# Expert outputs scattered to token order and summed per batch inside the next attention, in a four-layer decoder

## The chip, the cores and the metric

The kernel runs on one NeuronCore of a Trainium2 chip. The time is device time in microseconds for one execution of the whole program, from its first to its last instruction on that core.

## The reference, cut to what matters

The model is a decoder of four layers with layer norm after each sublayer: x = layernorm(x + f(x)) twelve times, for x of 8 batches, 256 tokens and width 256. In layers 0, 1 and 2 the sublayers are self attention, cross attention and a feed-forward network with experts. The change is about the experts of layers 0 and 1 and the attentions that follow them. Layer 0 sends each token to one of 8 experts and weights the result with the expert's softmax probability:

```python
sel = expert_idx == e
out = out + jnp.where(sel, expert_w, 0.0)[:, None] * y
```

Layer 1 sends each token to four of 32 experts. An expert takes at most C = 256 tokens; a choice that finds its expert full counts as zero. A shared expert is added.

```python
slot = jnp.minimum(pos, C)
expert_out = jnp.pad(expert_out, ((0, 0), (0, 1), (0, 0)))
gate = jnp.where(pos < C, w_s, 0.0)[:, None]
routed = jnp.zeros_like(x).at[t_s].add(expert_out[e_s, slot] * gate)
shared = _silu_and_mul(x @ shared_w_gate_up) @ shared_w_down
return (routed + shared).reshape(b, s, h)
```

## The kernel before

**Tiling.** The 2048 tokens are 16 tiles of 128 (NT = 16); a batch is two tiles. The residual X lies in SBUF as [128, 16, 256], beside xT, its transpose, from which the projections read. `finish(i)` closes a sublayer for the two tiles i and i+1: statistics (L163, L164), reciprocal square root, the normalised X (L187), four transposes on TensorE (L173) and a copy into xT by ScalarE (L174). The reciprocal square root is two POOL operations (L141, L143) within the attentions and cross attentions, where a flag `power` is set, and eleven tiny VectorE operations (L146 to L154, three Newton steps) within the expert layers.

**Order.** The program is written engine by engine through a tile framework with pools of buffers; a scheduler decides the order in which instructions stand on each engine, and inserts the waits. On each engine, instructions run in that order. Weights of the next sublayer are loaded one sublayer ahead into two tiles that alternate.

**l0_ffn** (lines 920 to 1015). After routing, tokens are grouped by expert into at most 23 blocks of 128 slots. Before it, in l0_xattn, X was written to a DRAM table `xd` by ScalarE's DMA queue (L851), batch by batch. For each block: POOL gathers the block's expert weights `we` (2.1 MB, two buffers) and its 128 token rows `xe` by indirect DMA (`gather_rows`, L893); TensorE multiplies; VectorE adds the bias to give `y` (L1005); SP writes `y` to the DRAM table `yd` in slot order (L1006). When all blocks are written, a second loop over the tiles gathers `yg`, the row of each token, from `yd` by POOL, weights it and adds X on VectorE (L1012), and calls `finish`.

**l1_ffn** (lines 1120 to 1195). `route1` (L1030 to 1117) makes `take`, the token of each expert's slot, by small matmuls against one-hot tables (`own`, `at`, `found`), and `slot`, the slot of each token's choice. Then the 32 experts: SP loads `we` (L1159, 384 KB), POOL gathers two tiles `xe`, TensorE transposes and multiplies, VectorE copies `y` (L1176), SP writes it to `yd` (L1177). `prepare_l2_xattn`, work for a later sublayer, is placed among the experts by the scheduler. When all experts are written, a loop over the 16 tiles adds the shared expert's product `py` to X (`acc`, L1187), gathers four `yg` rows per token by POOL and adds each with its weight on VectorE (L1192), and calls `finish` for two tiles at a time.

**attention16** (L593 on) runs l1_attn and l2_attn batch by batch: `pair(b)` projects two batches (`turned` L777 in l1_attn for rotary positions; `qv`, `kv`, `vp`), `largest16` finds score maxima (`low`, reductions on VectorE, L462 and L478), `lower16` (L497, L499) subtracts them, then exponentials on ScalarE, sums and output.

## Time and profile before

| | us |
|---|---|
| median of 3 runs | 2801.1 (2792.59 to 2802.07) |
| the profiled execution | 2675.02 |
| its span, first to last instruction | 2673.2 |
| PE, DVE, ACT, POOL busy | 2156.6, 1678.8, 957.6, 890.1 |

The profiled execution is 126 us shorter than the median of the three timed runs; its mean granted TensorE clock is 0.883. All stage times below are of that one execution. In the profile, PE is TensorE, DVE VectorE, ACT ScalarE, POOL GpSimd and SP the engine that only issues DMAs. A group row names line, engine, operation, output and inputs, the count, the busy time and the mean of one, then the engine's idle time just before such instructions and what ended most of it. A row of waits names the waiting engine and line, what it waited for, total us, times, and the longest. Stages by their first and last instructions: l0_ffn's blocks 332 to 557.6, its gathers and norms to 594, l1_attn from there; l1_ffn's experts 1026 to 1173.4, its gathers to 1257, l2_attn from there.

### The profile page before, as it was taken

What the parts mean: (1) busy time and instruction counts of PE and PEld (TensorE: products, weight loads), DVE (VectorE), ACT (ScalarE), POOL (GpSimd) and SP (SyncE); (2) the same over time, 40 slices, a digit from 0 to 9 for tenths busy, and PEclk for the clock granted to TensorE, in tenths of its full rate; (3) what the DMA queues carried; (4) which work ended last, traced back from release to release, by engine and by line L of the source; (5) the groups of instructions that cost most, each with busy time, mean ns of one, the idle gap of its engine ahead of it and who ended that gap; (6) DMA issues with size and microseconds to landing.
All of it is one profiled execution on the core that took longest, in us unless ns stands there. A gap on an engine that the chain in (4) does not pass through costs nothing.

```text
span 2673.2 us, 40915 instructions
## 1 busy us (share of the span) xinstructions
PE 2156.6 (81%) x14331; PEld 1560.5 (58%) x14331; DVE 1678.8 (63%) x5710; ACT 957.6 (36%) x2197; POOL 890.1 (33%) x949
## 2 busy tenths in 40 slices
PE   8978688869999867854998667888898899878975
PEld 5555477745556546741555425666677677656754
DVE  4754400056666757536676788787797787664876
ACT  2321133323333344211344224345455445433431
POOL 1021121131111112446111003776767766670000
PEclk9998599989998877985999788898999998887987
DMA  2001276720001013743000001212111211220000
GB/s 84 2 1 36 88 255 242 268 76 1 1 1 68 13 43 99 229 147 87 1 1 25 36 0 60 54 52 53 51 48 46 59 46 50 54 75 0 1 20 12
DMA packets 84172, 166.28 MB, mean 62 GB/s; under 512 B 31653, under 2 KB 51253, under 8 KB 80256
## 3 DMA queue, kind: packets, MB, share of 16 engines
q0 software_dynamic: 52288, 110.51, 13.5%
q1 hardware_dynamic: 28924, 49.45, 5.5%
q10 hardware_dynamic: 2756, 3.72, 0.4%
q8 instruction: 114, 1.87, 0.3%
q14 instruction: 90, 0.74, 0.1%
HBM read 242.90 MB, written 17.70 MB: 97 GB/s over the span
## 4 chain that ended last, share of the span: by engine, by line
PE 20%; DVE 17%; DMA 6%; issue 5%; POOL 2%; ACT 2%; POOLq 0%; ACTq 0%; DVEq 0%
DMA rows<-in_l2f_table_dram,index 6%; PE s L132 3%; PE pp L132 3%; PE po L1392 3%; PE po L132 3%; DVE junk L1340 2%; DVE low L478 1%; POOL rows L893 1%; PE ph L132 1%; PE sc L132 1%; PE s L1538 1%; PE sc L445 1%; PE s L1516 1%; DVE X L187 1%; DVE top_i L1216 1%
## 5 line engine op out<-in xcount | busy, mean ns | idle before, releaser
L893 POOL DMA_INDIRECT rows<-in_l2f_table_dram,index x512 | 531.9, 1039 | 227.7 <-issue 68.9
L1340 DVE SCALAR_TENSOR_TENSOR junk<-rows,X 128x256 f32<-128x256 f32 x512 | 215.8, 421 | 145.7 <-DMA rows<-in_l2f_table_dram,index 134.6
L1392 PE MATMUL po<-rows,diag 128*128 128x256 f32 x768 | 218.5, 423 | 43.6 <-ACT diag L1391 41.6
L132 PE MATMUL ph<-xeT,we 128*128 128x128 f32 x1248 | 187.4, 294 | 35.2 <-DMA we<-in_l0f_experts_dram,wrow 31.0
L132 PEld LDWEIGHTS ph<-xeT,we 128*128 128x128 f32 x1248 | 172.8, 204 | 58.5 <-DMA we<-in_l0f_experts_dram,wrow 34.4
L1392 PEld LDWEIGHTS po<-rows,diag 128*128 128x128 f32 x768 | 149.0, 207 | 91.3 <-ACT diag L1391 65.0
L553 POOL TENSOR_TENSOR aT<-sides,inv 128x256 f32<-128x256 f32 x64 | 46.7, 730 | 448.4 <-DVE sides L551 255.8
L132 PE MATMUL pp<-xT,w 128*128 128x256 f32 (+1 forms) x672 | 183.4, 411 | 9.6 <-DVE hT L1028 3.3
L173 PE MATMUL pt<-ident,X 128*128 128x128 f32 x352 | 77.7, 335 | 119.7 <-DVE X L187 105.5
L1391 ACT ACTIVATE diag<-ident,dots 128x128 f32<-128x128 f32 x384 | 133.1, 394 | 103.0 <-DVE dots L1386 62.7
L893 POOL DMA_INDIRECT xe<-xd,take x87 | 85.0, 977 | 221.7 <-DVE y L1005 94.7
L132 PEld LDWEIGHTS pp<-xT,w 128*128 128x128 f32 x672 | 131.9, 203 | 40.2 <-issue 9.4
L174 ACT COPY xT<-pt 128x512 f32<-128x512 f32 x88 | 51.5, 586 | 277.0 <-PE pt L173 276.7
L1005 DVE TENSOR_TENSOR y<-py,we 128x256 f32<-128x256 f32 x23 | 9.8, 425 | 220.3 <-PE py L132 220.3
L141 POOL TENSOR_SCALAR rs_v<-ln_mv 128x2 f32<-128x2 f32 x48 | 12.4, 259 | 389.2 <-DVE ln_mv L164 358.5
L173 PEld LDWEIGHTS pt<-ident,X 128*128 128x128 f32 x352 | 50.2, 165 | 156.7 <-issue 73.3
L132 PE MATMUL py<-we,hT 128*128 128x256 f32 x496 | 132.2, 391 | 0.9 <-DVE hT L1028 0.9
L517 ACT ACTIVATE e<-sc 128x512 f32<-128x512 f32 (+1 forms) x155 | 82.0, 602 | 105.5 <-PE sc L445 92.2
L999 ACT ACTIVATE hT<-ph,we 128x128 f32<-128x128 f32 x184 | 66.0, 367 | 142.8 <-PE ph L132 136.0
L187 DVE TENSOR_SCALAR X<-z,ln_mv,rs_y 128x256 f32<-128x256 f32 x192 | 72.0, 418 | 52.2 <-POOL rs_y L143 52.1
L445 PE MATMUL sc<-kv,qv 32*128 32x128 f32 (+2 forms) x1448 | 101.5, 320 | 2.8 <-DVE sides L551 0.8
L445 PEld LDWEIGHTS sc<-kv,qv 32*128 32x128 f32 x1448 | 78.3, 190 | 37.4 <-issue 30.1
(489 smaller groups left out, 5223.5 us busy)
## 6 DMA issues: line engine op xcount, KB each, us to landing
we<-in_l1f_experts_dram SPq DMA_DIRECT2D x32, 384.0 KB, 4.2
yd<-y SPq DMA_DIRECT2D x32, 256.0 KB, 2.1
rows<-in_l2f_table_dram,index POOLq DMA_INDIRECT x512, 2.8
w<-in_l2x_w_dram SPq DMA_DIRECT2D x1, 4096.0 KB
yd<-y SPq DMA_DIRECT2D x23, 128.0 KB, 1.7
X<-in_x_dram SPq DMA_DIRECT2D x8, 256.0 KB, 7.7
xd<-X ACTq DMA_DIRECT2D x8, 256.0 KB, 2.2
xd<-X SPq DMA_DIRECT2D x8, 256.0 KB, 2.1
```

Of the source, the lines that this page charges most:

```text
L132: self.nc.tensor.matmul(out, lhsT=lhsT, rhs=rhs, start=n == 0, stop=n == last and bias is None)
L173: nc.tensor.transpose(pt[:, c, j, :], self.X[:, i0 + j * step, c * P : (c + 1) * P], self.ident)
L174: nc.scalar.copy(self.xT4[:, :, i0 : i0 + step + 1 : step, :], pt)
L187: nc.vector.tensor_scalar(self.X[:, i, :], z[:, j, :], mv[:, j, 0:1], r[:, j : j + 1], ALU.subtract, ALU.mult)
L445: nc.tensor.matmul(sc[: shape[0], part], lhsT=lhsT, rhs=rhs, start=mask is None, stop=True, skip_group_check=True)
L517: lambda r, sc: nc.scalar.activation(e0[m][:n0, r], sc, AF.Exp),
L553: nc.gpsimd.tensor_tensor(out, split(both), split(inv), ALU.mult)
L893: self.nc.gpsimd.indirect_dma_start(out=out, out_offset=None, in_=table, in_offset=bass.IndirectOffsetOnAxis(ap=index, axis=0), **({} if r ...
L999: nc.scalar.activation(hT[:, g + f, :], ph[:, f, :], AF.Gelu, bias=b1[:, g + f : g + f + 1])
L1340: nc.vector.scalar_tensor_tensor(junk, row, 1.0, self.X[:, i, :], ALU.mult, ALU.mult, accum_out=out)
L1391: nc.scalar.activation(diag, self.ident, AF.Copy, scale=dots[:, k : k + 1])
L1392: nc.tensor.matmul(po, lhsT=diag, rhs=rows[:, k, D:], start=False, stop=g + k == H * K - 2)
```

## The change

The two tables of results are now laid out by token and choice: yd0 has a row per token, yd1 four rows per token. In both expert layers each `y` is scattered to its rows by POOL as soon as it exists. The slots that hold no token get an index beyond the table, and are dropped by a bounds check. The index `put` comes from `take`; in layer 1 the number of the choice is added, for which `own` gets a third table and `found` a third column. SP's writes of `y` and the loops of gathers go away. In l1_ffn the shared expert is added to X in eight steps (L1250 after). The weighted sums and `finish` move into the attention that follows: `ready(b)` loads a batch's rows in order with one DMA (256 KB in l1_attn with three buffers, 1 MB in l2_attn with two), adds them on VectorE (L978 after; two operations a batch in l1_attn, eight in l2_attn), and finishes the batch. It is called for batches 0 and 1 ahead of the first projection, for 2 after it, and for b+3 in each batch. As dropped choices leave rows of yd1 unwritten, l1_attn fills yd1 with zeros at its start, by one memset (L786) and 16 DMAs of 512 KB from SP (L788). The expert weights `gw` and the buffers lie in the spare part of the attention's weight tile. Lines of the kernel after differ from those of before: L502 after is L499, L806 is L777, L1089 is the scatter of l0_ffn, L1242 that of l1_ffn.

```diff
@@ class Net
+        self.yd0 = dram.tile([NTOK, D], F32, name="yd0")
+        self.yd1 = dram.tile([NTOK * 4, D], F32, name="yd1")
@@ attention16
+        for b in range(2 if ready else 0):
+            ready(b)
         pair(0)
+        if ready:
+            ready(2)
...
         for b in range(B):
             ahead = []
+            if ready and b + 3 < B:
+                ready(b + 3)
@@ l2_attn
+                ready=self.taken_back(self.yd1, 4, self.gw1, spare, 2, pool_from=8),
@@ l1_attn
+        zero = spare[:, 10 * D :]
+        nc.vector.memset(zero, 0.0)
+        for i in range(NT):
+            nc.sync.dma_start(
+                self.yd1[i * 4 * P : (i + 1) * 4 * P, :].rearrange("(p k) d -> p k d", k=4),
+                zero.unsqueeze(1).to_broadcast([P, 4, D]),
+            )
...
+ready=self.taken_back(self.yd0, 1, self.gw0, spare, 3)
@@ new functions
+    def scatter_rows(self, table, index, src):
+        ins = self.nc.gpsimd.indirect_dma_start(
+            out=table,
+            out_offset=bass.IndirectOffsetOnAxis(ap=index, axis=0),
+            in_=src,
+            in_offset=None,
+            bounds_check=table.shape[0] - 1,
+            oob_is_err=False,
+        ).ins
...
+    def put_index(self, takef, n, keep, per=1, part=None):
+        none = keep.tile([P, n], F32, name="none_at")
+        nc.vector.tensor_scalar(none, takef, 0.5, 1e6, ALU.is_lt, ALU.mult)
+        if part is not None:
+            nc.vector.tensor_tensor(none, none, part, ALU.add)
+        nc.vector.scalar_tensor_tensor(none, takef, float(per), none, ALU.mult, ALU.add)
+        put = keep.tile([P, n], U32, name="put")
+        nc.vector.tensor_scalar(put, none, float(per), 0.0, ALU.subtract, ALU.max)
+        return put
+    def taken_back(self, yd, k, gw, spare, nbuf, pool_from=B):
+        def batch(b):
+            y, z = ys[:, b % nbuf], zs[:, b % 2]
+            nc.sync.dma_start(
+                y, yd[b * S * k : (b + 1) * S * k, :].rearrange("(j p k) d -> p j k d", p=P, k=k)
+            )
+            engine = nc.gpsimd if b >= pool_from else nc.vector
+            for j in range(2):
+                t = 2 * b + j
+                for n in range(k):
+                    acc = z[:, j] if n else self.X[:, t, :]
+                    engine.scalar_tensor_tensor(
+                        z[:, j], y[:, j, n], gw[:, t, n : n + 1], acc, ALU.mult, ALU.add
+                    )
+            self.finish(2 * b, 1, z)
@@ l0_ffn
-                    nc.sync.dma_start(yd[n * P : (n + 1) * P, :], y)
-                for i in range(0, NT, 2):
-                    z = work.tile([P, 2, D], F32, name="z")
-                    for j in range(2):
-                        y = work.tile([P, D], F32, name="yg")
-                        self.gather_rows(y, yd, slot[:, i + j, :])
-                        nc.vector.scalar_tensor_tensor(
-                            z[:, j], y, gw[:, i + j : i + j + 1], self.X[:, i + j, :], ALU.mult, ALU.add
-                        )
-                    self.finish(i, 1, z)
+                    self.scatter_rows(self.yd0, put[:, n : n + 1], y)
@@ route1
+        for k in range(K):
+            nc.scalar.mul(own[:, k, 2], oh[:, k], float(k))
...
+        put = self.put_index(takef, 2 * E, keep, K, choice)
@@ l1_ffn
-                    nc.sync.dma_start(yd[e * C : (e + 1) * C, :].rearrange("(t p) d -> p t d", p=P), y)
+                    for n in range(2):
+                        self.scatter_rows(self.yd1, put[:, n * E + e : n * E + e + 1], y[:, n])
...
-                for i in range(0, NT, 2):
-                    z = work.tile([P, 2, D], F32, name="z")
+                for t in range(0, NT, 2):
+                    po = ps.tile([P, 2, D], F32, name="py")
                     for j in range(2):
-                        t = i + j
-                        po = ps.tile([P, 2, D], F32, name="py")
-                        self.mm(po[:, 0, :], [(shT[:, t * P : (t + 1) * P], sd)])
-                        acc = work.tile([P, D], F32, name="acc")
-                        nc.vector.tensor_tensor(acc, po[:, 0, :], self.X[:, t, :], ALU.add)
-                        for k in range(K):
-                            y = work.tile([P, D], F32, name="yg", bufs=6)
-                            self.gather_rows(y, yd, slot[:, t, k : k + 1])
-                            out = z[:, j] if k == K - 1 else acc
-                            nc.vector.scalar_tensor_tensor(out, y, gw[:, t, k : k + 1], acc, ALU.mult, ALU.add)
-                    self.finish(i, 1, z)
+                        self.mm(po[:, j, :], [(shT[:, (t + j) * P : (t + j + 1) * P], sd)])
+                    x = self.X[:, t : t + 2, :]
+                    nc.vector.tensor_tensor(x, po, x, ALU.add)
```

## The prediction

> **What bounds the kernel now.** I read the span cut into windows first, with the edges at the stages that the change touches: the expert blocks of l0_ffn, what follows them, the expert loop of l1_ffn, its gathers, the start of l2_attn, the rest of it. Columns: start:end length, busy time of each engine with instructions in brackets, granted clock, DMA share, GB/s.
>
> ```profile
> 332.00:557.60 225.60, 192.44 (x1148) 170.84 (x1148) 9.74 (x23) 73.76 (x208) 39.23 (x42) 0.93 0.67 243
> 557.60:578.00 20.40, 3.19 (x9) 1.87 (x10) 13.36 (x70) 1.17 (x2) 11.95 (x13) 0.61 0.27 79
> 1047.40:1173.40 126.00, 108.46 (x758) 95.44 (x756) 63.34 (x121) 29.74 (x91) 55.88 (x59) 0.99 0.73 216
> 1173.40:1257.40 84.00, 24.74 (x61) 12.11 (x59) 49.86 (x190) 3.52 (x6) 60.96 (x64) 0.54 0.36 102
> 1286.00:1480.00 194.00, 162.00 (x1814) 99.64 (x1815) 129.30 (x283) 79.84 (x142) 26.88 (x39) 0.96 0.06 22
> ```
>
> The expert loop is TensorE's: 31 periods from the first y (1047.5) to the last (1173.4), 4.06 us each, PE busy 86%, POOL 44%. The 84 us behind it belong to POOL: 64 gathers, PE nearly idle. The 20 us behind l0_ffn's blocks are the same in small. Next, the groups and waits of that 84 us stretch, to see the price of a gather, and who waits.
>
> ```profile
> L893 POOL DMA_INDIRECT yg<-yd,slot x64 | 61.0, 953 | 31.3 <-DMA yd<-y 12.1 <-issue 5.8 <-DVE rs_y L154 3.0
> L1192 DVE SCALAR_TENSOR_TENSOR acc<-yg,gw,acc 128x256 f32<-128x256 f32 x47 | 22.7, 483 | 31.5 <-DMA yg<-yd,slot 31.0
> ...
> PE pt L173 <- DVE X L187: 37.3, 6, 10.0
> ```
>
> A gather costs 0.95 us busy and 0.30 us between two: 64 x 1.25 = 80 us. VectorE waits 31 us for them, TensorE 37 us for VectorE. Last, a timeline of the expert loop, which tells how long an expert takes from its gather to its y.
>
> ```profile
> 1102.20 0.97 POOL L893 DMA_INDIRECT xe<-xd,take  x1 [1.12 <-DMA xe<-xd,take]
> ...
> 1106.67 0.41 PE L908 MATMUL pt<-ident,xe 128*128 128x128 f32 x2 [1.09 <-DMA xe<-xd,take]
> ...
> 1108.83 0.69 DVE L1176 COPY y<-py 128x512 f32<-128x512 f32 x1 [1.19 <-PE py L132]
> ```
>
> The tile gathered at 1102.20 is transposed at 1106.67, and the y that stands behind this transpose on PE is ready at 1109.5: 7.3 us.
>
> **What the Trainium skill says.** "DMA: Bandwidth & Descriptors", "Anatomy of one DMA — SWDGE (gpsimd) path": about 2.0 us and bytes/436 GB/s, so 2.3 us for 128 KB. The yg gathers land in 2.8 us, xe, beside weight loads, in 3.8 us: more, same order. The same page, "Issuing engines are not separate DMA queues": all DMAs share 16 engines, so the 8.4 MB zero fill takes time from whatever moves then; the trace of before has no such overlap. "SBUF — State Buffer", "SBUF: two separate sides": GpSimd and a VectorE operation with two SBUF inputs can lock each other out. It agrees in tendency: l2_ffn's bounds-checked gathers beside VectorE's two-input L1340 take 1039 ns in the mean, the yg gathers 953.
>
> ```profile
> L893 POOL DMA_INDIRECT rows<-in_l2f_table_dram,index x512 | 531.9, 1039 | 227.7 <-issue 68.9
> ```
>
> **The change, part by part.** (a) Zero fill of yd1: one memset and 16 SP DMAs of 512 KB from about 243 us. SP has nothing else then; DMA is 18% busy over 240 to 300. At the 243 GB/s of the block loop it takes 8.4 MB / 243 = 35 us. ACT's eight xd writes of l0_xattn come among them: in the order built, the last three writes and the zero row wait for the 11th to 13th part of the fill, due near 270 where they issue near 290. Cover: that slack, and xd is first read at 325; behind the fill on SP stand only the weights of l1_xattn. Cost 0; without the cover about 5 us.
>
> (b) l0_ffn's blocks: SP's 23 writes go, 23 scatters come on POOL. No scatter is in the trace of before. Its nearest row is the bounds-checked gather: 0.998 us median plus 0.30, so 1.30. Bounds: 1.25 as a plain gather (no reason for less, it makes the same 128 row addresses), 1.79 from the slowest of those 512 gathers, 1.487 us, and the gap. Each stands before the weight gather of block n+2, which frees a buffer only at y(n) as before; in most blocks the scatter takes the place of an xe gather (1.25) that moves behind it, in the last six or seven it comes on top. Two buffers alternate, so half counts: 6.5 x 1.30 x 0.5 = 4 us; at worst all, 22 x 1.30 x 0.5 = 14; at best 0.
>
> (c) l0 to l1: 16 gathers go; VectorE's Newton steps go too (finish is called inside l1_attn, which takes its root on POOL). Before, the last y is at 557.65 and the first `low` reduction of l1_attn at 607.07. After: y 561.7, scatter and landing 2.8, the 256 KB load 2.2 (as xd's writes of this size), so 567. Then VectorE stands first in line, in the order built: seven batches of two weighted sums (0.48 each), statistics 1.17 and X 0.8, 2.95 a batch, 20.7; turned and vp as before, 6.9; first low at 595. That is -12. The eighth batch's sums and two norms, 5 us, are left inside l1_attn, where I count half of it as hidden: +3. Sum -9, range -14 to +3.
>
> (d) Routing of l1_ffn: four ACT multiplies of 512 numbers come (0.59 each, from ACT's like rows) before 16 that `found` waits for, and a small DVE index computation before the first gather: +2. The five small DVE operations for slots were not on the path.
>
> (e) Expert loop: 32 SP writes go, 64 scatters come. POOL before: 57 gathers x 1.25 = 71 us in 126, waiting for PE. POOL after: per expert 2 x 1.25 + 2 x 1.31 = 5.1 us, over PE's 4.06, so **POOL becomes the bound**. The order built alternates two gathers, two scatters; a scatter waits for y, and behind it stand gathers of the experts two and three ahead. From a gather to the scatter of the y that depends on it POOL has one and a half periods, 7.6 us, of other work; the path is 7.3 us. So it just doesn't lock. From the first y at 1049.5: 28.5 experts x 5.12 = 146, last gather at 1195.5; landing 4, the y in front 2.5, its own expert 4, last y 1206; second scatter issued 1.3 later and landed 2.8 after that: 1210. The loop's end has moved by +35.
>
> (f) l1 to l2: 64 gathers go, eight loads of 1 MB come. Price of one: `we` of 384 KB lands in 4.2, `we` of 2.1 MB in 9.4, so 3 us and 3 us per MB, 6.2. First batch at 1216. X += shared (8 adds, 16 products) runs beside the last scatters. VectorE's order then puts 45 of the 64 weighted sums and five norms before the first `lower16` (L499): 45 x 0.484 = 21.8; 5 x 1.95 = 9.8; projection copies and lows as before, 14.1 busy; 3 for the root on POOL and for loads, which have two buffers. 1216 + 48.7 = 1265, against 1283.4 before: -18. The remaining 19 sums and three norms, 9.2 + 5.9 = 15 us, fall inside l2_attn, where VectorE is 67% busy with `low` on the path: about half hides, +7 (range 2 to 15). (d), (e) and (f): -11.
>
> Sum: -9 - 11 = **-20 us of the profiled execution**, 2675 to 2655. The median of the runs shown is 126 us above that execution, and nothing in the page says where; I carry the difference over unscaled: 2801 - 20 = 2781. If those runs are slower in TensorE's work, the POOL-bound loop hides some of it, a reason for a little more.
>
> **Rivals.** A, the loop stays TensorE's: were the 0.30 between POOL's instructions hidden, an expert would cost POOL 3.9 and the loop stay at 4.06; then the +35 goes, less 3 for the last scatter: 2801 - 20 - 32 = 2749. Against it: the yg gathers show the 0.30 each time. B, VectorE takes it back: the 15 us inside l2_attn all on the path (+8), and the two load buffers starve the sums (+6): 2795. For it: VectorE at 67% there with its reductions in the chain. C, slower, **POOL's period per expert**: the scatter that waits for y holds gathers behind it. The gain is gone at a period of 5.12 + 20/28.5 = 5.8, and the kernel is slower by 0.5% from 6.3. That takes scatters of 1.9 us, or a path from gather to y of 1.5 x 6.3 = 9.5 us in place of 7.3, as scatter writes crowd the 73% busy DMA engines. At 6.6 it gives 2781 + 42 = 2823. That the change doesn't do what it says is excluded for the gathers: they are gone from the order built.
>
> **How the numbers follow.** Forecast 0.43, A 0.15, B 0.22, C 0.20. About 0.5% (14 us) is what a measurement of this kernel can tell from no change. Faster: A, and two thirds of the forecast's own spread, 0.45; same: most of B and the rest, 0.32; slower: C and a tail of B, 0.23. The range reaches near A and near C, leaving out half of A and half of C: 2753 to 2818. The forecast's own range is 2768 to 2796.
>
> **What would show it.** Right: y's period in the expert loop 5.1 to 5.3 with POOL over 90% busy there; scatters of about 1.0 us; last y near 1206; first L499 of l2_attn (L502 after) near 1265; first low of l1_attn near 595; l0_xattn unchanged to 325. Wrong: a period near 4.1 (A) or above 5.8 (C), ACT waiting for the zero fill, or a gap on VectorE before the sums for loads.

## The result, and the profile after

| | before | after |
|---|---|---|
| median, us | 2801.6 (2792.6 to 2811.4, 4 runs) | 2835.2 (2832.9 to 2843.3, 4 runs) |
| ratio | | 1.013 [1.010, 1.016] |
| profiled execution; span | 2675.02; 2673.2 | 2833.34; 2831.6 |

The changed kernel is slower, by 1.3%. The two profiles must not be laid side by side: the kernel before takes 2679 us on some chips and 2804 us on others (medians of 9 to 61 runs on each of five chips: 2679.1 and 2679.3 on two, 2803.9, 2804.7 and 2805.8 on three). By their times, its profile came from the first kind and the timed runs from the second. Each chip was used in one session, so "kind of chip" may stand for something in its surroundings. The kernel before was profiled again on the second kind ("before again", the first experiment), and the stages below compare that profile with the one after. Its span is 137 us longer than in the first profile; 124 of these lie in l2_ffn, which the change doesn't touch: from its first to its last gather 747 us on one kind, 871 on the other. The windows of the kernel after, with its own edges and the columns of the prediction: l0_ffn's blocks, what follows them up to the last load, the expert loop from first to last y, from there to the first `lower16` of l2_attn, and l2_attn.

```profile
332.00:578.20 246.20, 198.11 (x1146) 177.35 (x1145) 9.73 (x23) 72.45 (x207) 60.80 (x62) 0.89 0.58 216
578.20:591.00 12.80, 1.54 (x6) 1.04 (x7) 5.77 (x20) 0.59 (x1) 6.78 (x9) 0.56 0.40 116
1068.20:1255.20 187.00, 130.51 (x766) 112.31 (x764) 65.73 (x122) 30.29 (x91) 121.51 (x122) 0.85 0.45 140
1255.20:1308.50 53.30, 33.65 (x161) 18.78 (x161) 45.08 (x110) 7.58 (x11) 13.35 (x18) 0.76 0.40 143
1310.00:1504.00 194.00, 172.61 (x1840) 105.81 (x1836) 130.35 (x298) 82.52 (x144) 26.98 (x40) 0.93 0.02 7
```

The same stages of the kernel before, on the second kind of chip:

```profile
332.00:558.60 226.60, 191.44 (x1142) 170.19 (x1140) 9.77 (x23) 71.83 (x205) 37.78 (x40) 0.93 0.66 237
1048.20:1178.60 130.40, 110.27 (x759) 97.11 (x757) 64.19 (x122) 29.73 (x91) 56.17 (x59) 0.97 0.73 209
1178.60:1300.40 121.80, 47.54 (x181) 23.99 (x181) 69.88 (x243) 11.51 (x17) 68.36 (x70) 0.59 0.26 72
```

The blocks take 20 us more. The expert loop takes 187 us in place of 130 for the same 32 experts, and POOL, which was to be its bound, is busy only 121.5 of them, 65%; with the 0.30 us between its instructions counted it is taken for 158 of them, 84%. The stretch behind the loop falls from 122 to 53 us. Landmarks from the trace give the whole account; the forecast's column is worked out from its own landmarks (the last y at 1206, `lower16` at 1265, and so on), each less that of before:

| stretch, us | before again | after | difference | forecast |
|---|---|---|---|---|
| l0_ffn, first to last y | 219.1 | 238.4 | +19.3 | +4 |
| to l1_attn's first `low` | 49.4 | 36.6 | -12.8 | -16 |
| l1_attn, its `low` stretch | 354.4 | 367.8 | +13.4 | +3 |
| to l1_ffn's first y | 86.0 | 85.6 | -0.4 | +2 |
| expert loop, first to last y | 130.2 | 186.9 | +56.7 | +31 |
| to the first `lower16` | 121.9 | 53.4 | -68.5 | -50 |
| l2_attn, to its last `low` | 160.1 | 178.6 | +18.5 | +7 |
| rest | | | -5.8 | 0 |
| sum | | | +20.4 | -20 |

By layers: layer 0 (the first three rows) was forecast to gain 9 us and lost 20; layer 1 (the next four) was forecast to gain 10 and lost 6. The profiles differ by 20 us and the medians by 34: the profiled execution of before again took 2812.5 us, 8.5 more than the median of its own runs, and single executions of the kernel after spread over 10 us, of before over 19. The new instructions on the page after:

```profile
L924 POOL DMA_INDIRECT xe<-xd,take x87 | 85.8, 986 | 181.1 <-PE pt L992 118.2
L936 POOL DMA_INDIRECT yd<-y,put x87 | 88.9, 1022 | 111.2 <-DVE y L1088 69.9
```

A scatter (L936) is busy for 1.02 us; with the 0.30 between two instructions, 1.32. The zero fill changed nothing that can be seen: the first y of l0_ffn is at 339.8 after and at 339.4 before.

### The profile page after: what moved, and what is told of

Its sections match the earlier page's. It is cut to its first block, busy times and chain, and to the rows that moved or that the text cites. A ratio compares the mean times of both kernels' runs of the same rounds, so it can differ in the third digit from the quotient of the medians.

```text
span 2831.6 us, 40750 instructions
## 1 busy us (share of the span) xinstructions
PE 2221.4 (78%) x14331; PEld 1612.7 (57%) x14331; DVE 1662.9 (59%) x5530; ACT 962.1 (34%) x2202; POOL 919.6 (32%) x988
## 4 chain that ended last, share of the span: by engine, by line
PE 27%; DVE 16%; issue 5%; another core or an unknown queue 3%; ACT 3%; POOL 2%; DMA 1%; ACTq 0%; POOLq 0%; DVEq 0%
PE po L1449 5%; PE pp L135 5%; PE s L135 4%; PE po L135 3%; DVE junk L1397 1%; PE po L1430 1%; DVE low L481 1%; PE ph L135 1%; PE s L1595 1%; PE s L1573 1%; PE sc L135 1%; DVE w L978 1%; DVE X L190 1%; PE sc L448 1%
## 5 line engine op out<-in xcount | busy, mean ns | idle before, releaser
L1449 PE MATMUL po<-rows,diag 128*128 128x256 f32 x768 | 233.8, 441 | 103.3 <-ACT diag L1448 54.1
L135 PE MATMUL ph<-xeT,we 128*128 128x128 f32 x1248 | 203.2, 312 | 74.0 <-DMA we<-in_l0f_experts_dram,wrow 46.4
L135 PEld LDWEIGHTS ph<-xeT,we 128*128 128x128 f32 x1248 | 190.1, 222 | 99.5 <-DMA we<-in_l0f_experts_dram,wrow 49.3
L1449 PEld LDWEIGHTS po<-rows,diag 128*128 128x128 f32 x768 | 154.8, 216 | 155.1 <-ACT diag L1448 71.5
L135 PE MATMUL pp<-xT,w 128*128 128x256 f32 (+1 forms) x672 | 195.8, 433 | 27.0 <-issue 15.8
L1448 ACT ACTIVATE diag<-ident,dots 128x128 f32<-128x128 f32 x384 | 134.8, 395 | 137.7 <-PE po L1449 56.7
L135 PEld LDWEIGHTS pp<-xT,w 128*128 128x128 f32 x672 | 140.6, 216 | 61.1 <-issue 24.1
L135 PE MATMUL py<-we,hT 128*128 128x256 f32 x496 | 141.1, 412 | 3.4 <-DVE hT L1102 3.4
L936 POOL DMA_INDIRECT yd<-y,put x87 | 88.9, 1022 | 111.2 <-DVE y L1088 69.9
L448 PE MATMUL sc<-qv,kv 32*128 32x128 f32 (+2 forms) x1396 | 102.1, 346 | 0.0
```

The lines of the kernel that those rows point to most:

```text
L135: self.nc.tensor.matmul(out, lhsT=lhsT, rhs=rhs, start=n == 0, stop=n == last and bias is None)
L448: nc.tensor.matmul(sc[: shape[0], part], lhsT=lhsT, rhs=rhs, start=mask is None, stop=True, skip_group_check=True)
L936: ins = self.nc.gpsimd.indirect_dma_start(out=table, out_offset=bass.IndirectOffsetOnAxis(ap=index, axis=0), in_=src, in_offset=None, boun ...
L1448: nc.scalar.activation(diag, self.ident, AF.Copy, scale=dots[:, k : k + 1])
L1449: nc.tensor.matmul(po, lhsT=diag, rhs=rows[:, k, D:], start=False, stop=g + k == H * K - 2)
```

## The experiments

### Before again, and each half alone

`before again` is the kernel before without an edit. `l0 only` keeps the old l1_ffn and l2_attn; `l1 only` keeps the old l0_ffn and l1_attn. Their core edits, against the kernel after:

```diff
 # l0 only: in l1_ffn, as before
-                    for n in range(2):
-                        self.scatter_rows(self.yd1, put[:, n * E + e : n * E + e + 1], y[:, n])
+                    nc.sync.dma_start(yd[e * C : (e + 1) * C, :].rearrange("(t p) d -> p t d", p=P), y)
 # l1 only: in l0_ffn, as before
-                    self.scatter_rows(self.yd0, put[:, n : n + 1], y)
+                    nc.sync.dma_start(yd[n * P : (n + 1) * P, :], y)
```

> The kernel before once more, unchanged. From l2_ffn on the kernel after has the same order of instructions on each engine as the kernel before, yet the profiled executions differ there by 114 us (the rows gathers take 747 us before, 860 us after). If that belongs to the execution and not to the change, this run's profiled execution takes about 2800 us, with 840 to 860 us between the first and the last rows gather, and reaches the first of them near 1652 us. If the change causes it, this run shows 747 us there again and some 2675 us in all.

> The change in layer 0 alone (scatter in the expert blocks of l0_ffn, sums inside l1_attn); layer 1 as before, no zero fill. My theory now: the blocks of l0_ffn lose 20 us (each scatter stands before the next weight gather), their tail gains 13, l1_attn loses some 8: 10 to 15 us slower than before, about 2813. Rival, the prediction on record: blocks lose 4, sum a gain of 9, about 2792.

> The change in layer 1 alone (two scatters per expert, zero fill in l1_attn, sums inside l2_attn); layer 0 as before. My theory now: the expert loop loses 60 us (period 6.0 in place of 4.06), the tail to the first lower16 of l2_attn gains 56, l2_attn loses 19: 20 to 28 us slower than before, about 2825. Rival, the prediction on record: loop loses 31, tail gains about 47, l2_attn loses 7: a gain of 10, about 2791.

Measured, all on one chip of the second kind: before again 2803.96, ratio 0.9999 [0.9976, 1.0022]; l0 only 2817.8, 1.0060 [1.0038, 1.0082]; l1 only 2809.1, 1.0027 [1.0005, 1.0048]. Each half loses, the second less than the 20 to 28 us that were expected, as the stretch behind its loop saves 68 us and not 56. The second kind of chip shows itself in `before again` much as expected, but its first gather of l2_ffn comes at 1669 and not at 1652: the stretch behind the expert loop is 12.5 us longer there too. `l0 only` loses all that l0_ffn and l1_attn lose together (its last y at 576.6, the end of l1_attn's `low` stretch at 980.9, in place of 558.5 and 962.3); `l1 only` has the expert loop of the change, 187.8 us.

### Where l0_ffn's 19 us come from

The order on POOL in one block, after and in `before again` (start, length, engine, line, operation, idle before):

```profile
406.89 0.95 POOL L924 DMA_INDIRECT xe<-xd,take  x1 [11.49 <-PE pt L992]
408.14 1.01 POOL L936 DMA_INDIRECT yd<-y,put  x1 [0.30 <-issue]
409.46 0.98 POOL L924 DMA_INDIRECT we<-in_l0f_experts_dram,wrow  x1 [0.30 <-issue]
```

```profile
400.58 0.94 POOL L893 DMA_INDIRECT xe<-xd,take  x1 [10.44 <-DVE y L1005]
401.83 0.94 POOL L893 DMA_INDIRECT we<-in_l0f_experts_dram,wrow  x1 [0.30 <-ACT hT L999]
```

After a y, POOL used to issue `xe`, then `we`; now the scatter stands between the two. From y(n) to the gather of `we`(n+2) it was 1.7 us in 15 blocks and 0.7 in six; it is 3.0 and 2.0, except in one block: 1.3 more, the price of the scatter (times from the start of y). To test it, `l0 late` issues the scatter of a block behind the weight gather of the block two ahead:

```diff
                     self.gather_rows(we, self.ins["l0f_experts"], wrow[:, n : n + 1])
+                    if n > 1:
+                        self.scatter_rows(self.yd0, put[:, n - 2 : n - 1], ys.pop(0))
...
-                    y = work.tile([P, D], F32, name="y")
+                    y = work.tile([P, D], F32, name="y", bufs=5)
                     nc.vector.tensor_tensor(y, py, b2, ALU.add)
-                    self.scatter_rows(self.yd0, put[:, n : n + 1], y)
+                    ys.append(y)
...
```

> The kernel after, with each scatter of l0_ffn written two blocks later, behind the weight gather of the block that takes over the buffer. If the scatter ahead of that gather is what slows the blocks, they take 219 us again from the first to the last y (238 in after, 219 before) and the kernel some 18 us less than after, about 2817. Rival: the blocks are slower because the scatters' writes share the DMA engines with the weight gathers; then they stay at 238 and the time at 2835.

Measured on a chip of the first kind: 2680.1, ratio 1.0000 [0.9989, 1.0012]. Its blocks take 221.8 us from first to last y, and 0.7 or 1.7 us from y to `we` as before:

```profile
401.33 0.97 POOL L924 DMA_INDIRECT xe<-xd,take  x1 [8.97 <-DVE y L1091]
402.61 0.95 POOL L924 DMA_INDIRECT we<-in_l0f_experts_dram,wrow  x1 [0.30 <-ACT hT L1085]
403.86 1.01 POOL L936 DMA_INDIRECT yd<-y,put  x1 [0.30 <-issue]
```

A kernel below with layer 0 as changed (`fill`) takes 238.8 for them on this kind of chip. So the place of one POOL instruction ahead of a 2.1 MB weight gather costs l0_ffn 17 us. The blocks as they were before take 215.8 us in the profile of before, and 219.0, 221.0 and 221.2 in three kernels below that leave them alone; so the scatter as such costs at most 6 us, and perhaps nothing. The rival, that the scatters' writes crowd the weight gathers, wanted 238. `l0 late` also has more buffers for y, but these are not the cause: in the kernel after all of y's waiting is for TensorE.

```profile
L1088 DVE TENSOR_TENSOR y<-py,we 128x256 f32<-128x256 f32 x23 | 9.8, 425 | 242.6 <-PE py L135 242.6
```

As nothing else differs, this gives an estimate for the kernel after on the first kind, where it was not run: 2680 and 17, 2697 us, some 18 over the kernel before.

### The expert loop: whose time is it?

`sp write` replaces layer 1's two scatters by one SP write in slot order; the loads then read rows of other tokens, so the sums are of other rows. `xe8` gives the gathered rows eight buffers in place of three (in both layers; the text of a later run says four).

```diff
 # sp write
-                    for n in range(2):
-                        self.scatter_rows(self.yd1, put[:, n * E + e : n * E + e + 1], y[:, n])
+                    nc.sync.dma_start(self.yd1[e * C : (e + 1) * C, :].rearrange("(t p) d -> p t d", p=P), y)
 # xe8
-        xe = work.tile([P, D], F32, name="xe")
+        xe = work.tile([P, D], F32, name="xe", bufs=8)
```

> The kernel after, with the two scatters of an expert replaced by one SP write of y in slot order, as before; the sums inside l2_attn read these rows (so they add other rows than the reference's). If the scatters on POOL are what slows the expert loop, its period goes back to 4.06 us and the kernel is some 60 us faster than after, near 2775, and faster than before by 25. Rival: the loop is slowed by the added work around it (shared DMA engines, sums), then the period stays above 5 and the time near 2835.

> The kernel after, with eight buffers for the gathered tiles xe in place of three, so that POOL may gather more tiles ahead of the scatters. Four POOL instructions of an expert follow each other in 5.24 us, the period is 6.0. If the rest is the chain from a gather over its transpose to the y for which the scatter waits, the period comes to 5.2 to 5.4 and the kernel gains some 20 us on after, about 2814. Rival: the pauses come from elsewhere (weights, TensorE), and the period stays at 6.0.

`sp write`, second kind: 2775.5, ratio 0.9915 [0.9886, 0.9945], 60 us below the kernel after. Its loop:

```profile
1068.20:1202.30 134.10, 110.91 (x764) 97.67 (x762) 64.93 (x122) 29.92 (x91) 56.07 (x60) 0.97 0.74 220
```

134 us, with DMA busy at 0.74: the scatters, not the rest of the change, cost the loop its 53 to 57 us, and crowded DMA engines are not how (0.45 with the scatters). On the first kind, `l0 late`, which leaves this loop as the change has it, and then `xe8`:

```profile
1052.40:1216.60 164.20, 117.03 (x761) 102.54 (x763) 65.56 (x122) 30.29 (x91) 121.22 (x122) 0.94 0.51 159
```

```profile
1059.80:1211.80 152.00, 117.80 (x760) 103.64 (x762) 64.97 (x122) 28.61 (x91) 114.89 (x117) 0.88 0.55 166
```

164 us is 5.3 us an expert, and 152 is 4.9: there POOL is near its bound of 5.2 (2 x 1.29 + 2 x 1.32), as forecast. With the 0.30 us between instructions it is taken for 157 of the 164 us, and 150 of the 152; with eight buffers five more of the gathers lie ahead of the first y. `xe8` as a whole: 2678.0, ratio 0.9995 [0.9978, 1.0011]. It keeps most of l0_ffn's loss (232.0 us for its blocks), and gains 12 us in the loop in spite of one new wait: POOL, now far ahead with gathers, comes late to a small reduction that VectorE needs.

```profile
1103.44 0.15 DVE L1690 TENSOR_SCALAR vis_step<-vis_all 128x1 f32<-128x1 f32 x1 [15.70 <-POOL vis_all L1682]
```

So the second kind of chip adds some 20 us to the same loop. The kernel after was run twice more to see whether that holds.

> The changed kernel once more, without any edit, beside the kernel before on one chip. Theory: what differs between a chip where the kernel before takes some 2680 us and one where it takes some 2804 us is the period of the expert loop under the change, 5.3 against 6.0 us; so on the quicker one the ratio is 1.003 (2685 to 2692 us, loop 164 us from first to last y), on the slower one 1.013 (2840 us, loop 187 us). Rival: the loss of 60 us in the loop belongs to the change itself, and the ratio is 1.012 or more on either.

> The changed kernel without any edit, for the chip on which it and the two below run. Where the kernel before takes 2680 us: loop of 161 to 166 us without late results of TensorE, ratio 1.003 to 1.006. Where it takes 2804 us: loop of 185 to 187 us, 30 us or more of late results, ratio 1.009 to 1.013. Rival (the loop of 187 us is one chip's own): anything between.

Both came on chips of the second kind: 2829.2, ratio 1.0086 [1.0057, 1.0115], loop 184.7; and 2833.9, ratio 1.0101 [1.0070, 1.0132], loop 183.4. On the first kind the unedited kernel was not run.

### What the second kind of chip does in the loop

A slower landing of DMAs does not show: from issue to landing it is 3.6 us for `xe` and 2.5 for a scatter in `l0 late`, 2.9 and 3.1 in `xe8` (medians, first kind). On the second kind most of a DMA's 16 semaphore writes are missing from the traces; the 15 gathers and 5 scatters of the loop after that have all of theirs took 3.0 and 2.45 us in the mean. ("DMA: Bandwidth & Descriptors" of the Trainium skill, "Anatomy of one DMA — SWDGE (gpsimd) path", gives an estimate of 2.3 us for 128 KB; the order of size agrees, and most landings here take longer.) What differs is when TensorE's results are taken. `silu` is ScalarE's activation, the first reader of an expert's `ph`. The timeline of the kernel after in one such place, TensorE, ScalarE, VectorE's y and POOL's gathers:

```profile
1154.32 1.03 PE L135 MATMUL py<-we,hT 128*128 128x256 f32 x4
1155.19 1.50 PE L135 MATMUL ph<-xeT,we 128*128 128x128 f32 x12
...
1158.19 0.69 DVE L1240 COPY y<-py 128x512 f32<-128x512 f32 x1 [1.98 <-DMA xe<-xd,take]
1158.47 0.41 PE L992 MATMUL pt<-ident,xe 128*128 128x128 f32 x2 [1.56 <-DMA xe<-xd,take]
...
1163.87 0.38 ACT L1101 ACTIVATE silu<-ph 128x256 f32<-128x256 f32 x1 [8.87 <-remote]
1164.15 0.64 ACT L994 COPY xeT<-pt 128x256 f32<-128x256 f32 x2
1164.15 1.02 POOL L924 DMA_INDIRECT xe<-xd,take  x1 [1.44 <-remote]
...
1164.57 1.22 PE L135 MATMUL ph<-xeT,we 128*128 128x128 f32 x4 [4.50 <-ACT xeT L994]
```

The same place in `l0 late`, on the first kind:

```profile
1149.97 1.72 PE L135 MATMUL ph<-xeT,we 128*128 128x128 f32 x14
1150.17 0.69 DVE L1245 COPY y<-py 128x512 f32<-128x512 f32 x1 [0.41 <-DMA yd<-y,put]
1151.53 0.38 PE L992 MATMUL pt<-ident,xe 128*128 128x128 f32 x2
1151.73 0.39 ACT L1106 ACTIVATE silu<-ph 128x256 f32<-128x256 f32 x1 [2.73 <-PE ph L135]
```

There, silu starts 0.04 us after the recorded end of its last `ph` matmul. Here y starts 2.8 us after the recorded end of `py`, and silu 7.2 us after that of `ph` (1156.69). ScalarE goes on at 1163.87, POOL, which waits for the transposes to free a buffer, at 1164.15: both waited for TensorE, whose matmuls are recorded as done. The ends of matmuls are modelled by the profile; the semaphore writes with which TensorE tells of a result are recorded by themselves, and they do come late. In `l0 late` each of the 134 of the loop comes within 0.02 us of the recorded end, and in `before again` all 115 that its trace holds come within 0.05. In the loop after, 48 of the 108 held come more than 0.05 us behind the last end. In the place above `py` is told of at 1158.16 and `ph` at 1163.84, 0.03 us before their readers start. Counted over the loops (silu's start, less the later of the last `ph` end and the end of ScalarE's instruction before it; those over 0.6 us):

| kernel | kind of chip | loop, us | late silus | sum, us |
|---|---|---|---|---|
| before; before again | first; second | 127; 130 | 0; 0 | |
| sp write | second | 134 | 0 | |
| l0 late; xe8 | first | 164; 152 | 0; 0 | |
| after; again; third | second | 187; 185; 183 | 10; 9; 11 | 31; 35; 30 |
| l1 only | second | 188 | 10 | 32 |

In those of over 3 us, twelve or fourteen `ph` matmuls, recorded with 1.3 to 1.6 us in all, lie between a y and the next silu, which are 4.3 to 5.7 us apart (1.6 in the place on the first kind): a mean pace of a quarter to a third of the full rate. It is not an even pace: the two pairs of transposes behind the `ph` above are told of at 1163.89 and 1163.93, 0.04 us apart, where on the first kind two that follow each other are 0.22 apart (1148.27 and 1148.49 in `l0 late`). So the results were held and then let go together; the trace doesn't show whether TensorE itself stood still. The records of the granted clock do not account for it, they say 1.00 up to 1160 and then 0.5. "TensorE: Matmul & The Clock Gate" of the Trainium skill, "Part 1: The HAM clock gate", warns that on trn2 the clock's trace events "have been observed to be unreliable", and that the clock has been seen stuck at a quarter for 50 us and more. The mean pace here would fit a quarter, but the late stretches last under 8 us and end with results close together; no record here shows the clock at a quarter.

What calls it forth? One theory says TensorE's pauses, which POOL's longer loop makes (24 to 27 of over 0.8 us in the loop after; on the first kind 23 in `l0 late`, without harm). Rivals: TensorE's load, or the scatters' writes. Three kernels were made for this.

`one scatter` leaves out the second scatter of each expert, so that half of the rows of results count as zero. `fill` puts idle matmuls into the pauses. `idle gathers` takes the kernel before and adds two gathers that nothing reads, each behind a small copy from y, where the change has its scatters.

```diff
 # one scatter
-                    for n in range(2):
+                    for n in range(1):
                         self.scatter_rows(self.yd1, put[:, n * E + e : n * E + e + 1], y[:, n])
 # fill
-                    xeT = [self.gathered_T(xd, take[:, n * E + e : n * E + e + 1], work) for n in range(2)]
                     ph = ps.tile([P, 2, 256], F32, name="ph")
+                    xeT = []
+                    for n in range(2):
+                        nc.tensor.matmul(ph[:, n, :], lhsT=self.ident, rhs=self.consts[:, :256], start=True, stop=True)
+                        xeT.append(self.gathered_T(xd, take[:, n * E + e : n * E + e + 1], work))
 # idle gathers, in the kernel before
                     nc.sync.dma_start(yd[e * C : (e + 1) * C, :].rearrange("(t p) d -> p t d", p=P), y)
+                    for n in range(2):
+                        junk = work.tile([P, D], F32, name="junk")
+                        nc.vector.tensor_copy(junk[:, :1], y[:, n, :1])
+                        self.gather_rows(junk, xd, take[:, 2 * e + n : 2 * e + n + 1])
```

> The changed kernel with only the first of the two scatters of each expert in layer 1's loop; the results of the other half of the tile are left unwritten, so that half of the rows are summed as zeros. Theory: POOL's instructions are the bound of the loop; three of them take 3.9 us in place of 5.2, the period falls to that of the kernel before, 4.1 to 4.4, the loop lasts 130 to 137 us, and the time is 30 us below the changed kernel on the quicker chip, 50 to 60 on the slower. Rival: the wait of a scatter for its y, which stays, sets the period; the loop stays over 150 us.

> The changed kernel with one idle matmul of 256 columns ahead of each pair of transposes in layer 1's expert loop, its result overwritten by the expert's own. It makes TensorE busier by some 1.0 us an expert (4.1 to 5.1) and shortens its pauses. Where the kernel before takes some 2804 us: theory, the results of TensorE that come late in the loop (9 or 10 times, 31 to 35 us in the loop) follow upon TensorE's pauses; with fewer and shorter pauses they fall below 15 us, the loop from 185 to 187 us to 165 to 172 us, and the time is 10 to 20 us below the changed kernel. Rival: they follow upon TensorE's load, or come from the scatters themselves; they stay at 30 us or more, and the loop lasts 187 us or longer. Where the kernel before takes 2680 us there are none, and both expect a loop of 164 to 172 us.

> The kernel before, with its own writes and gathers, and besides, for each expert of layer 1, two gathers into tiles that nothing reads, each behind a small copy from the expert's y: they stand where the change has its scatters and wait for the same y, but write nothing to DRAM. The order on POOL is two gathers of rows, two idle ones, as with the change. Theory (POOL's place in the loop): the loop's period is that of the change, 5.0 to 5.3 us where the kernel before takes 2680 us, and 5.7 to 6.1, with late results of TensorE of 20 us or more in the loop, where it takes 2804 us. Rival (the scatters' writes): no late results, and a period of 5.0 to 5.3 on either.

> The kernel before with two idle gathers behind each y of layer 1 (nothing scattered), on another chip. Before, where the kernel before takes 2679 us, its loop took 173 us and had no late results of TensorE. Where the kernel before takes 2804 us: theory (pauses of TensorE), late results of 20 us or more in the loop, which lasts 190 to 200 us; rival (the scatters' writes), no late results and a loop of 170 to 175 us. Where it takes 2680 us again: 173 us for both.

> The changed kernel with idle matmuls in the pauses of the expert loop of layer 1, on another chip. Before, where the kernel before takes 2679 us, its loop took 161 us. Where it takes 2804 us: theory (pauses), late results below 15 us and a loop of 165 to 172 us; rival (load, or the scatters), 30 us or more and 187 us or longer. Where it takes 2680 us again: 161 us for both.

`one scatter`, second kind: 2790.9, ratio 0.9958 [0.9942, 0.9975], 38 us below the kernel after on the same chip, where 50 to 60 were expected. Its loop takes 146 us, 4.7 an expert; the bound of three POOL instructions is 3.9, and POOL is busy 62% (80% with the 0.30 between instructions). That lies between the 130 to 137 us of the theory and the 150 of its rival, in a profile of the fastest of 18 executions. Late silus: 8, together 11 us. The loop falls by 39 us, about what the 31 missing instructions take (31 x 1.32 = 41), but both from above POOL's bound: POOL's time is what is paid for, and it is not all that is paid.

`idle gathers` took 2720.2 (ratio 1.015 [1.012, 1.018]) on the first kind, with a loop of 173 us and no late silu; on the second kind 2855.1 (1.019 [1.014, 1.024]), a loop of 185 us and 10 late silus of 18 us in all.

```profile
1035.90:1220.90 185.00, 127.53 (x757) 109.74 (x755) 70.29 (x183) 29.99 (x91) 114.43 (x121) 0.89 0.65 190
```

Nothing is scattered there. The scatters' writes are thus not needed: POOL instructions that wait for y, two an expert, give both the long loop and the late results. (18 us is a little under the 20 that were named; the loop of 173 us is 5.6 us an expert, over the 5.0 to 5.3 expected there, and 185 is under the 190 to 200 that the theory of pauses named.)

`fill` took 2716.3 (1.011 [1.007, 1.015]) on the first kind, loop 161 us, no late silu; on the second 2849.6 (1.018 [1.013, 1.024]), loop 185 us, 10 late silus of 33 us in all:

```profile
1064.10:1249.60 185.50, 142.83 (x868) 122.15 (x867) 43.93 (x84) 32.21 (x91) 119.59 (x120) 0.93 0.45 141
```

The theory of pauses wanted a loop of 165 to 172 us and late results below 15: it is not borne out, though pauses of over 0.8 us fell from 24 or more to 16. (The 33 us count from each expert's own `ph` matmuls, as in the table. Counted from the idle matmuls that stand behind them, for the next expert, they are 23.) This is what the rival named, load or the scatters, within the spread of the unedited kernel; the scatters are out by `idle gathers`, and load was not varied by itself. One thing besides moved in `fill`: the scheduler put two reductions of `prepare_l2_xattn` behind the loop (at 1253 and 1269 us, which in the kernel after are at 1118 and 1154), and the stretch to `lower16` grew from 53 to 72 us. That is about what it is slower by as a whole. What makes TensorE's results late on this kind of chip stays open.

### The sums inside the attentions

VectorE in one of the first batches of l1_attn after; the moved norm's work is L166 and L190 on `w`, the sums L978:

```profile
660.18 1.29 DVE L465 TENSOR_REDUCE low<-sc 128x4 f32<-128x512 f32 x2 [3.58 <-PE pt L448]
...
664.05 0.39 DVE L166 BATCH_NORM_STATS2 ln_st<-w 128x6 f32<-128x256 f32 x1
...
667.69 0.73 DVE L190 TENSOR_SCALAR X<-w,ln_mv,rs_y 128x256 f32<-128x256 f32 x2 [1.14 <-POOL rs_y L146]
668.34 0.87 DVE L978 SCALAR_TENSOR_TENSOR w<-w,X 128x256 f32<-128x256 f32 x2
669.13 0.68 DVE L481 TENSOR_REDUCE low<-sc 128x2 f32<-128x512 f32 x1
...
678.29 1.41 DVE L502 SCALAR_TENSOR_TENSOR qv<-sc,consts,qv 128x512 f32<-128x512 f32 x2 [1.91 <-PE sc L500]
```

The same in `before again`:

```profile
653.51 1.29 DVE L462 TENSOR_REDUCE low<-sc 128x4 f32<-128x512 f32 x2 [3.14 <-PE pt L445]
...
659.41 0.69 DVE L478 TENSOR_REDUCE low<-sc 128x2 f32<-128x512 f32 x1
...
666.44 1.41 DVE L499 SCALAR_TENSOR_TENSOR qv<-sc,consts,qv 128x512 f32<-128x512 f32 x2 [0.65 <-PE sc L497]
```

Between the first and the second reduction of one batch VectorE, in order, now does a norm and two sums and waits 1.14 us for POOL's root: 8.95 us in place of 5.90. To `lower16` it is 18.1 in place of 12.9, 5 us more. Each of the first three batches loses about that (41.6 us for 36.0, 24.0 for 19.2, 41.3 for 36); the later ones, with nothing moved in, lose nothing. l2_attn shows the same, from one first `lower16` to the next: 36.4 for 29.6, 24.6 for 19.6, 34.1 for 29.0. l1_attn takes some 10 us less in some executions, with nothing changed in it (344.7 to 354.4 in profiles of the second kind); `one scatter`, in such an execution, has 356.9 with the change, so the loss is 12 to 13 us in either.

Two kernels go another way: SP writes in slot order as before, and the gathers, sums and norms moved into the attentions (`lazy`, both layers; `lazy l1`, layer 1 alone).

```diff
 # in taken_back
-            nc.sync.dma_start(
-                y, yd[b * S * k : (b + 1) * S * k, :].rearrange("(j p k) d -> p j k d", p=P, k=k)
-            )
+            for j in range(2):
+                for n in range(k):
+                    self.gather_rows(y[:, j, n], yd, slot[:, 2 * b + j, n : n + 1])
```

> Results written by SP in slot order as before, no scatter, no zero fill; the gathers, sums and norms of a batch called from inside the attention that follows, in both layers. Against the kernel before: expert loops as before; the tail of l1_ffn saves 60 us (two batches' gathers instead of eight stand before the first projection), l2_attn loses 18 or a little more, the tail of l0_ffn saves 10 and l1_attn loses 13: about 2765. Rival: the gathers on POOL inside l2_attn (10 us a batch of 24) hold up its POOL and VectorE work, and l2_attn loses 40: about 2790.

> The same in layer 1 alone, layer 0 as in the kernel before. If the moved norms of layer 0 cost in l1_attn what they save behind l0_ffn, this is within 5 us of the variant with both layers, about 2763. Rival: layer 0's move pays, then this one is 10 us slower than the other.

First kind: 2697.5, ratio 1.0070 [1.0042, 1.0098], and 2688.1, 1.0035 [1.0023, 1.0047]. A gain of 14 to 39 us had been expected. The loop is short again (130 us), but from the last y to `lower16` it is still 104 us, against 109 before, and l2_attn loses 18 to 19 us, as with the change. The reason lies in the order: the scheduler put 63 of the 64 gathers of layer 1 ahead of the first `lower16`, and 49 of the 64 sums. So these runs show that this order gains nothing; gathers spread over the attention were not tested.

### A version that is faster than both

`l1 xe8` keeps layer 0 as before and has the change in layer 1, with eight buffers of gathered rows in both. `l1 xe8 late` calls `ready(b + 3)` at the end of a batch, and `l1 xe8 fill` adds the idle matmuls.

```diff
 # l1 xe8 late, in attention16
         for b in range(B):
             ahead = []
-            if ready and b + 3 < B:
-                ready(b + 3)
...
+            if ready and b + 3 < B:
+                ready(b + 3)
```

> The change in layer 1 alone, layer 0 as before, with eight buffers of gathered rows (xe) in layer 1's expert loop in place of four. Theory: the loss in layer 0 (some 14 us of the median) is avoided and the loop is held by POOL's four instructions alone, 4.9 us an expert; ratio 0.996 (10 us faster than before; between 0.993 and 0.998). Rival: whatever is gained ahead of the second attention is given back inside it, ratio 0.999 to 1.003.

> As the run before it, with the sums and the norm of batch b+3 called at the end of batch b of the attention, and no longer at its start. Theory: VectorE is in order and these instructions stand in the chain of the reductions wherever they are put; the attention's first batches lose the 18 us at other places, and the time is within 4 us of the run before it. Rival: their place among the reductions is what costs, and the time falls by 6 to 12 us.

> The same idle matmuls in the kernel that has the change in layer 1 alone and eight buffers of gathered rows, which took 0.9974 of the kernel before where that took 2806 us, with a loop of 182 us. Theory (pauses): the loop falls to 160 to 168 us and the ratio to 0.990 to 0.994. Rival (load, or the scatters): the loop stays at 180 us or more, ratio 0.997 to 1.001.

`l1 xe8`, second kind: 2797.2, ratio 0.9974 [0.9960, 0.9987], some 9 us faster than before, with a loop of 182 us and 12 late silus of 44 us: the buffers, which brought 12 us on the first kind, bring little in this loop. The ratio fell where it was expected, but not for the reason given: the loop was to take 4.9 us an expert and took 5.9. Up to `lower16` it is 32 us ahead (1268.1, against 1300.4), and gives 16 back in l2_attn. But of the 32, 6 stand already at l1_attn's first `low` (602.2, against 607.9), where nothing but layer 0's buffers is changed, and 16 at the first y of the expert loop (1032.5, against 1048.3), with the 10 us by which l1_attn varies. So what layer 1's change brings by itself on this kind of chip is next to nothing. `l1 xe8 late`: 2807.2, 1.0008 [0.9993, 1.0023]; l2_attn takes 185.8 us in place of 175.7. Both sides had it wrong: the place matters by 10 us, and the later one is worse. `l1 xe8 fill`, first kind: 2672.3, 0.9970 [0.9959, 0.9981], loop 149 us, no late silu; as it met the first kind, it does not test the theory of pauses. Its blocks of l0_ffn take 209.1 us, for 215.8 to 221.2 with three buffers: the whole gain of 7 us, or more. A gain of 0.3% is all that was measured, and it may be the buffers' alone: the kernel before with eight buffers and nothing else was not run. On the first kind layer 1's change may bring more: in `xe8` loop, stretch and l2_attn take 384.6 us together for 395.1 before. `l1 xe8` without idle matmuls was not run there.

## Why the prediction was wrong

It said 2781 and got 2835, beyond its range and on the other side. Most of its mechanisms are there; four costs in the sum were too small (the scatter in l0_ffn's blocks, the sums inside each of the two attentions, the expert loop), and one saving larger than said. The table above has each; against the forecast the errors are +15, +3, +10, -2, +26, -18, +11 and -6, which but for rounding make the 40 us between -20 and +20. The other 14 of the 54 us between the medians lie in which executions were profiled. By layers the error is 29 us in layer 0 and 16 in layer 1, so most of it lies in layer 0 and not around the expert loop.

**Right.** The price of a scatter (1.30 said, 1.32 measured), the zero fill at nothing, routing within 2 us, POOL as the new limit of the loop, and the order of size of what the gathers' removal saves. Behind the loop, 68 us were saved, where 50 were said: before, that stretch takes 122 us on the second kind of chip and 109 in the profile that the forecast was made from; after, it is 53, where 59 were said.

**(b) failed in its count.** "In most blocks the scatter takes the place of an xe gather (1.25) that moves behind it": it does not. The `xe` gather stayed ahead of the weight gather and the scatter came on top, 1.3 us later in all but one of 21 blocks, not in 6.5. It cost 0.9 us a block (19.3 / 22), two thirds of 1.3, where half was counted, in a third of the blocks. The upper bound of 14 us was exceeded by 5; `l0 late` shows the place as the cause. Why two thirds count and not half stays open.

**(c) and (f) failed in "about half hides".** The moved norms lie in the middle of VectorE's chain of reductions, and each brings a wait for POOL's root with it. l1_attn lost 13 us for 3, l2_attn 18 for 7. For l1_attn the timeline shows the place; for l2_attn the periods of its batches do. That another place gives another loss (10 us, `l1 xe8 late`) speaks for order as the cause, not for a mere sum of work.

**(e) was mis-sized, and partly for a reason that no profile of before could show.** POOL's bound of 5.2 us is met on the first kind of chip (5.3 measured, 5.12 said, +37.6 us for +31). On the kind on which the kernels were timed it is 5.9 to 6.0. There POOL stands idle, beyond the 0.30 between instructions, for 29 us in the loop, where it is 7 in `l0 late`: `POOL yd L936 <- DVE y L1240` stands at 16.9 us, and gathers wait another 13 for TensorE's `pt` or for what the profile can't name. That this comes of TensorE's late results fits every run (no long loop of the second kind without them), but no run takes the lateness away by itself on one chip. So "it just doesn't lock", with 7.3 us of path in 7.6, had no room for that. A period above 5.8, which it named as a sign of being wrong, is what came. Its sign of being right, POOL over 90% busy, could not come by its own prices: 3.9 us busy in 5.1 is 76%.

**Rival C** gave the right sign and named the right place, the period per expert, and the wait of the scatter for y. Its causes did not occur: scatters cost 1.02 and not 1.9 us, they land in 2.5 to 3.1 where the traces tell it, and the DMA engines are busy 0.45 and not more than 0.73. Its threshold of 6.3 was not reached; the kernel is slower at 6.0, as layer 0 and the two attentions took what was to pay for the loop. A is excluded: the 0.30 between POOL's instructions stays (median 0.305 in the loop). B, VectorE's chain, is part of what happened: the two attentions lost 32 us, 22 more than forecast, where B added 8 (and 6 for loads).

**The carry-over failed too.** The 126 us between the profile and the median were carried over "unscaled", with the thought that a slower TensorE would hide some of a POOL-bound loop. The opposite holds: the slower kind of chip made this loop longer by 20 us, and that of the kernel before by 3. That alone doesn't turn the sign: by the estimate above the kernel after loses some 18 us on the first kind too.

**One reading of the trace is not borne out.** The longer gathers of l2_ffn, 1039 ns against 953, were read as a tendency of GpSimd and VectorE to lock each other out. The yg gathers stand beside a two-input operation as well (L1192 in the prediction's own lines), and have no bounds check; so the two figures don't show a lock.

## What to carry to other kernels

An instruction put on a queue that feeds large transfers delays each transfer behind it by its own length (1.3 us here, which cost 0.9 us a block), so ask which DMA it is issued ahead of, and put it behind that one. Work that was moved into the chain of one in-order engine cost its whole length here, 5 us a batch, though VectorE had been busy only 67% of the stage; look at the instruction before and after the new place, not at the busy share. After such a move, look also where the scheduler has put the work (63 of 64 gathers had not moved behind the start of the attention). And where a profile and the timed runs differ by 5%, find out first where they differ, by a second profile of the kernel before: a loop at its limit may behave differently there.

## What was not expected of the hardware

- The same kernel takes 2679 us on some chips and 2804 on others. In l2_ffn of the kernel before, TensorE, ScalarE and VectorE are idle together for more than 1 us at a time in 29 places on the second kind, about 75 us in all, and in 3 places, 4 us, on the first.
- In the expert loop with the change, results of TensorE come up to 7.3 us after the recorded end of their matmuls, on three chips of three of the second kind and on none of the first (two chips). TensorE's own semaphore writes are as late, and often come 0.04 us apart. In the kernel after the granted clock reads 1.00 at the start of each of the ten waits, and in seven until the end. It happens with idle gathers in place of scatters and with filled pauses; it did not happen on the second kind in the three loops that TensorE bounds (`before again`, `sp write`, `l0 only`).
- Sixteen DMAs of 512 KB, issued together, cost nothing that could be measured beside the cross attention of layer 0.
